# Weights in DRAM by tap column: long writes and short reads in a convolution with involution

## The chip, the cores and the metric

The kernel runs on one core of a Trainium2 chip. The metric is the device time of one execution in microseconds, lower being better. The number to be predicted is the median over runs of the changed kernel.

## The reference

The input x has 32 images of 256 channels and 32 x 32 pixels. Two layers follow each other, each added to its own input:

```python
# layer 0: 3x3 convolution over group-normalised x, quantised to 10 mantissa bits
x = x + conv3x3(quantise(gn(x)), quantise(w0)) + bias
# layer 1: involution, 7x7, 16 groups of 16 channels
xn = gn(x)
y = relu(bn(w1 @ xn))             # 64 channels
w = w2 @ y + b2                   # per pixel: 16 groups x 49 taps
x = x + sum over k of w[g, k] * patch(xn)[g, c, k]
```

The second layer has different weights at every pixel, made from that pixel itself. `gn` has 32 groups of 8 channels.

## The kernel before

An image passes through five stages.

1. `front` normalises it, runs the 3x3 convolution in float16 on TensorE (L320, 18 matmuls for each half of the pixels and of the channels), adds bias and input on VectorE, normalises again into `xn` (L269), multiplies by w1 into PSUM (`py`, L368), and ScalarE turns that into `y_sb` (L375), which holds one image in one of two buffers. Then it transposes `xn` pixel by channel (L383) into `pixels`.
2. `weights` multiplies y by w2 for four rows of pixels at a time (L398). VectorE adds b2 and writes the result into the ring `w_sb` (L416). There, a partition is a pixel's column (and a pair of tap columns), and the free dimension runs over image rows, groups and tap rows.
3. `scatter` writes the weights from `w_sb` to the DRAM buffer `wd`, one DMA for each of the seven tap columns and each block of eight rows (L465, on SyncE's queue). `wd` is laid out by row and pixel: a pixel's weights for all seven tap columns lie together, so a DMA writes runs of WB = 160 floats, 640 bytes.
4. `load_bands` reads `wd` back into one of three `band` buffers, so that the partition is now a pixel (eight rows by 16 columns). It takes 16 DMAs for each block of eight rows, one for each of 16 columns (L478); each reads runs of a whole pixel, WPIX = 1124 floats, 4496 bytes, for two sides of the image. One in eight goes to SyncE's queue, the others to GpSimd's (POOL in the profile).
5. `sums` multiplies `pixels` by `band` (L503). The result in `acc` is what each pixel gives to the 7x7 window around it, and `add_windows` adds it to x on VectorE (L519). `store` writes the finished half image (L524).

Sizes: K = 4 blocks of eight rows per image, SIDES = 2, JC = 16 columns to a side. WINC = 22 columns of weights stand in a band for 16 pixels, WINI = 19 of them inside the image.

The order is written out by hand. A loop runs over steps; an image has 16, two for each of its M = 8 pieces, and every stage is called at its distance from the sums. `front` is a generator that goes on by one `yield` per step, and it starts 56 steps ahead. `weights` comes 18 steps ahead, `scatter` 17, `load_bands` 9 steps. Engines take their instructions in that order, each its own. The DMAs of a queue use eight semaphores in turn, so that a DMA waits for the one eight before it on its queue to land.

Of the kernel before, what the change touches and what calls it, by code (L numbers as in the profile page):

```python
# [9 lines left out]
F32 = mybir.dt.float32  # L10
AF = mybir.ActivationFunctionType
ALU = mybir.AluOpType

P = 128
B, C, H, W = 32, 256, 32, 32
N = H * W
# [3 lines left out]
K0, PAD0 = 3, 1  # L20
K1, PAD1 = 7, 3
TAPS = K1 * K1
CR = 64
G = 16
# [12 lines left out]
XR = 4  # L37
RG = 2
KP = P // RG
TR = RG * XR  # L40
SIDES = 2
JC = W // SIDES
K = H // TR
M = K * SIDES
WIN = XR + K1 - 1
WINC = JC + K1 - 1
WINI = JC + PAD1

WB = G * WIN
WPIX = K1 * WB + XR
SW = K1 * G
S = H + 2 * PAD1
T = 4
TW = P // T
PAIR = 3 * GC
PAIRS = G // 2
ROW = S * WPIX  # L60
WR = 4
NBAND = 3
SHARE = 8
NPIX = 6
# [7 lines left out]
def tile_quant_conv_then_involution(  # L72
# [16 lines left out]
    nc = tc.nc  # L89
    PSUM = bass.MemoryType.PSUM  # L90

    const = ctx.enter_context(tc.tile_pool(name="const", bufs=1))
# [3 lines left out]
    dram = ctx.enter_context(tc.tile_pool(name="dram", bufs=1, space=bass.MemoryType.DRAM))  # L96
# [37 lines left out]
    for t in sum(sum(sums_sb, []), []):  # L134
        nc.gpsimd.memset(t, 0.0)

    y_sb = [const.tile([P, N // 2], F32, name=f"y_{i}") for i in range(2)]
    bands = [const.tile([P, SIDES, WINC * WB + XR], F32, name=f"band_{i}") for i in range(NBAND)]
    for t in bands[CH:]:
        nc.gpsimd.memset(t, 0.0)  # L140
    pixels = [const.tile([P, 2, PAIRS, PAIR], F32, name=f"pixels_{i}") for i in range(NPIX)]
# [3 lines left out]

    w_sb = const.tile([P, 2, RING, G, WIN], F32, name="w_sb")
    nc.vector.memset(w_sb, 0.0)  # L147
    wd = dram.tile([H, S, WPIX], F32, name="wd")
    acc = [ps_acc.tile([P, RG, NT], F32, name=f"acc_{d}") for d in range(SIDES)]

    wq = const.tile([P, CH, K0 * K0, C], F16, name="wq")
    for kh in range(CH):
        wf = bands[kh].rearrange("p d n -> p (d n)")[:, : K0 * K0 * C].rearrange("p (k c) -> p k c", c=C)
        nc.sync.dma_start(wf, w0[kh * P : (kh + 1) * P])
        nc.vector.tensor_scalar(wq[:, kh], wf, F16_MAX, -F16_MAX, ALU.min, ALU.max)
        nc.gpsimd.memset(bands[kh], 0.0)
# [20 lines left out]
    bn_scale = const.tile([P, 1], F32, name="bn_scale")  # L177
    nc.vector.tensor_mul(bn_scale, bn[:, 0:1], bn_r)
    bn_shift = const.tile([P, 1], F32, name="bn_shift")
# [1 line left out]
    nc.vector.tensor_sub(bn_shift, bn[:, 1:2], bn_shift)  # L181


    for col, cols, at, n in (
        (0, S, K1 * WB, XR),
        (PAD1, PAD1, 0, PAD1 * WB),
        (W, PAD1, (K1 - PAD1) * WB, PAD1 * WB),
    ):
        to = bass.AP(
            tensor=wd.tensor,  # L190
            offset=wd.offset + col * WPIX + at,
            ap=[[ROW, H], [WPIX, cols], [1, n]],
        )
        nc.sync.dma_start(to, bands[NBAND - 1][:H, 0, :n].unsqueeze(1).to_broadcast([H, cols, n]))

    class GroupNorm:

# [77 lines left out]
    def front(b):  # L275
# [4 lines left out]
        def stages(n):  # L280
            for _ in range(n):
                yield

        gn = GroupNorm(b, 0)
# [18 lines left out]
        gn = GroupNorm(b, 1)  # L303
        gn.begin(N // NT)
        units = [(nt, mh) for nt in range(N // NT) for mh in range(CH)]
        for s in range(4 * len(units) + 2):
            u, i = divmod(s, 4)
            if u < len(units):
# [3 lines left out]
                for n in range(sum(CONV[:i]), sum(CONV[: i + 1])):  # L312


                    k = n if n < K0 * K0 else CH * K0 * K0 - 1 - n
                    kh, k = n // (K0 * K0), (k + K0 * K0 // 2) % (K0 * K0)
                    di, dj = k // K0 - PAD0, k % K0 - PAD0
                    r0, r1 = max(nt * RT, -di), min((nt + 1) * RT, H - di)
# [9 lines left out]
            u, i = divmod(s - 3, 4)  # L328
            if 0 <= u < len(units) and i < 3:
                nt, mh = units[u]  # L330
                cols = slice(nt * NT, (nt + 1) * NT)
# [22 lines left out]
        for h in range(CH):  # L354
            yield
            to = xn[:, h].rearrange("p (k d r j) -> p d k r j", d=SIDES, r=TR, j=JC)
            at = xt[:, h].rearrange("p (k r d j) -> p d k r j", d=SIDES, r=TR, j=JC)
            gn.apply(h, [(to[:, d], at[:, d]) for d in range(SIDES)])
        yield from stages(2)

        py = ps_m.tile([P, NT], F32, tag="m", name="py")
        for r0 in range(0, H, WR):
            cols = slice(r0 // 2 * W, (r0 + WR) // 2 * W)
            for kh in range(CH):
                px = xn[:, kh].rearrange("p (k d r j) -> p k r d j", d=SIDES, r=TR, j=JC)[:, r0 // TR]
                for i in range(2):
                    r = r0 % TR + 2 * i
# [4 lines left out]
                        start=kh == 0,  # L372
                        stop=kh == CH - 1,
                    )
        nc.scalar.activation(y_sb[b % 2], py, AF.Relu, bias=bn_shift, scale=bn_scale)  # L375
        yield from stages(5)

        for m in range(0, M, 2):
            yield
# [6 lines left out]
            to = pixels[(b * M + m) // 2 % NPIX].rearrange("p i a (v c) -> p (i a) v c", c=GC)  # L386
# [3 lines left out]
    def weights(b, r0):  # L390

        pws = [ps_w.tile([P, 2, 2, SW], F32, tag=f"pw{i}", name=f"pw{i}") for i in range(2)]
        for r in range(2):
            for t in range(T):
                for i in range(2):
                    half = slice(i * CR, (i + 1) * CR)
                    dj = slice(2 * t, min(2 * t + 2, K1))
                    nc.tensor.matmul(  # L398
                        pws[i][t * TW : (t + 1) * TW, r, : dj.stop - dj.start],
                        y_sb[b % 2][half, (r0 // 2 + r) * W : (r0 // 2 + r + 1) * W],  # L400
                        w2_sb[half, dj],
                        start=True,
                        stop=True,
                    )
        for i in range(2):
            for e in range(2):
                p = P if e == 0 else (K1 // 2) * TW
                for r, rows, d0, d1, at in ring_pieces(b, r0 + 2 * i):

                    to = w_sb[:p, e]  # L410
                    to = bass.AP(
                        tensor=to.tensor,
                        offset=to.offset + at * WB + K1 - 1 - d0,
                        ap=[to.ap[0], [WB, rows], [WB - 1, d1 - d0], [WIN, G]],
                    )
                    nc.vector.tensor_tensor(  # L416
                        to,
                        pws[i][:p, r : r + rows, e, d0 * G : d1 * G].rearrange("p r (d g) -> p r d g", g=G),
                        b2_sb[:p, e, d0 * G : d1 * G]
                        .unsqueeze(1)  # L420
                        .to_broadcast([p, rows, (d1 - d0) * G])
                        .rearrange("p r (d g) -> p r d g", g=G),
                        ALU.add,
                    )
# [29 lines left out]
    def scatter(b, k):  # L454

        at = (b * H + k * TR) % RING
        for dj in range(K1):
            t, e = divmod(dj, 2)
            to = bass.AP(
                tensor=wd.tensor,  # L460
                offset=wd.offset + k * TR * ROW + dj * WPIX + (K1 - 1 - dj) * WB,
                ap=[[WPIX, TW], [ROW, TR], [1, WB]],
            )
            rows = w_sb[t * TW : (t + 1) * TW, e, at : at + TR]
            nc.sync.dma_start(to, rows.rearrange("p s g r -> p s (g r)"))  # L465

    def load_bands(b, k):

        band = bands[(b * K + k) % NBAND]
        for i in range(JC):  # L470
            j = i // 2 + i % 2 * JC // 2
            src = bass.AP(
                tensor=wd.tensor,
                offset=wd.offset + k * TR * ROW + (j + PAD1) * WPIX,
                ap=[[ROW - 1, TR], [JC * WPIX, SIDES], [1, WPIX]],
            )
            queue = nc.sync if i % SHARE == SHARE - 1 else nc.gpsimd
            queue.dma_start(band[j::JC, :, j * WB : j * WB + WPIX], src)  # L478

    def windows(b, m):  # L480

# [7 lines left out]
    def sums(b, m):  # L489

        k, d = divmod(m, SIDES)
        j0 = 0 if d else PAD1
        band = bands[(b * K + k) % NBAND][:, d]
        px = pixels[(b * K + k) % NPIX][:, d]
        for h in range(CH):
            for v in range(2):
                for g, at, top, f, l in windows(b, m):
                    p = slice(g * KP, (g + 1) * KP)
                    of = band[p, g * XR + j0 * WB : g * XR + (j0 + WINI) * WB]
                    of = of.rearrange("p (j g r) -> p j g r", g=G, r=WIN)  # L500
                    for t in range(T):
                        a = h * T + t
                        nc.tensor.matmul(  # L503
                            at[t * TW : (t + 1) * TW, h, :, f - top : l - top],
                            px[p, a, v * GC : v * GC + TW],
                            of[:, :, 2 * a + v, f - top : l - top],
                            start=(h, v) == (0, 0),
                            stop=(h, v) == (CH - 1, 1),
                        )
# [25 lines left out]
    with tc.manual_schedule():  # L535
        fronts = {}
        for n in range(FRONT, B * per + 2):
            b, i = due(n, FRONT)
# [10 lines left out]
            b, i = due(n, 0)  # L549
            if b is not None and i % 2 == 0:  # L550
                sums(b, i // 2)
            b, i = due(n, 1)
# [6 lines left out]
            b, i = due(n, 2)  # L559
            if b is not None and i == 2 * (M - 1 - SIDES):  # L560
                store(b, 0)
            b, i = due(n, -LEAD)
# [3 lines left out]
            b, i = due(n, -LEAD + 1)  # L566
# [4 lines left out]
            b, i = due(n, LOAD)  # L571
# [3 lines left out]
            b, i = due(n, 3 - 4 * NBAND)  # L575
# [39 lines left out]
```

## Time and profile before

| | |
|---|---|
| median of 3 runs | 1402.68 us (1398.28 to 1410.33) |
| profiled execution | 1416.45 us |
| its span | 1414.7 us |
| granted TensorE clock, mean | 0.978 |
| TensorE busy | 1265.2 us (89%) |
| VectorE busy | 933.0 us (66%) |
| ScalarE busy | 729.8 us (52%) |
| GpSimd (POOL) busy | 1003.5 us (71%) |
| moved by DMA | 369.33 MB in 366232 packets |

In the profile PE is TensorE, PEld its loading of weights, DVE VectorE, ACT ScalarE, POOL GpSimd, SP SyncE. L478 is line 478 of the kernel. A q behind an engine means its queue, which waits and issues. In the table of DMA queues, q1 is what SyncE issues (scatters, an eighth of the band loads, loads and stores of x), and q0 is what GpSimd issues (the other band loads). Each line gives packets, megabytes, and the time that the packets took as a share of the time of all 16 DMA engines. A wait is given as who waited for whom, with the total in microseconds, the number of times and the longest.

### The profile page before, as it was taken

How to read it: one execution, taken by the hardware profiler on the slowest of the kernel's cores; microseconds unless marked ns; L12 is line 12 of the kernel's file. 1: busy time of each engine (PE TensorE's matmuls, PEld its weight loads, DVE VectorE, ACT ScalarE, POOL GpSimd, SP SyncE). 2: the span in 40 equal slices, each digit the busy share in tenths (PEclk: the TensorE clock that was granted, in tenths of full speed). 3: DMA queues.
4: the chain of work that ended last, by engine and by line, in shares of the span. 5: the costliest groups of instructions: out<-in, count | busy, mean ns of one | idle time of the engine just before them, and what ended most of it. 6: DMA issues, size and time to landing. Idle time of an engine off the chain costs nothing.

```text
span 1414.7 us, 70076 instructions
## 1 busy us (share of the span) xinstructions
PE 1265.2 (89%) x29440; PEld 802.2 (57%) x29440; DVE 933.0 (66%) x3180; ACT 729.8 (52%) x1699; POOL 1003.5 (71%) x1817
## 2 busy tenths in 40 slices
PE   4899899999999899989999999999999999999665
PEld 1456565566565566655566556565566556655543
DVE  4567667767677677766767667767667676766642
ACT  5775555455555445555545555554556454553300
POOL 7067767686776777767777777677776767777774
PEclk9999999999999999999999999999999999999976
DMA  6099899999999999999999999999999999999995
GB/s 212 6 228 283 251 277 276 281 262 285 277 273 264 287 268 269 294 260 270 289 267 287 268 277 253 273 280 273 274 289 271 268 279 282 278 270 262 258 258 165
DMA packets 366232, 369.33 MB, mean 261 GB/s; under 512 B 78624, under 2 KB 308192, under 8 KB 365664
## 3 DMA queue, kind: packets, MB, share of 16 engines
q1 hardware_dynamic: 279904, 235.72, 57.2%
q0 software_dynamic: 86016, 129.14, 34.5%
q8 instruction: 234, 3.83, 1.2%
q14 instruction: 78, 0.64, 0.1%
HBM read 183.81 MB, written 180.74 MB: 258 GB/s over the span
## 4 chain that ended last, share of the span: by engine, by line
PE 47%; DMA 31%; issue 7%; POOL 5%; DVE 4%; ACT 3%; SPq 2%; POOLq 0%; DVEq 0%; ACTq 0%
DMA band<-wd 24%; PE pc L320 19%; PE acc L503 15%; PE pw L398 9%; DMA wd<-w_sb 7%; POOL band L478 5%; PE py L368 3%; DVE w_sb L416 2%; PE pt L383 2%; SPq L465 2%; ACT junk L210 1%; DVE x L519 0%; DVE w_sb L147 0%; ACT xn L269 0%; DVE q L334 0%
## 5 line engine op out<-in xcount | busy, mean ns | idle before, releaser
L478 POOL DMA_DIRECT2D band<-wd x1792 | 978.0, 548 | 397.8 <-DMA band<-wd 249.0
L416 DVE TENSOR_TENSOR w_sb<-pw,b_sb 128x16 f32<-128x16 f32 (+9 forms) x1920 | 454.0, 350 | 386.9 <-PE pw L398 363.2
L320 PE MATMUL pc<-xq,wq 128*128 128x496 f16 (+3 forms) x2304 | 536.5, 379 | 31.3 <-ACT xq L269 21.4
L503 PE MATMUL acc<-band,pixels 64*32 64x190 f32 (+1 forms) x16384 | 420.5, 323 | 78.9 <-DMA band<-wd 39.6
L503 PEld LDWEIGHTS acc<-band,pixels 64*32 64x32 f32 x16384 | 298.3, 108 | 171.1 <-issue 101.5
L320 PEld LDWEIGHTS <-wq 128*128 128x128 f16 x2304 | 206.4, 98 | 328.9 <-issue 114.6
L398 PE MATMUL pw<-w_sb,y 64*32 64x224 f32 (+1 forms) x8192 | 296.6, 333 | 31.1 <-issue 29.4
L519 DVE TENSOR_TENSOR x<-acc,x 128x380 f32<-128x380 f32 (+1 forms) x512 | 261.7, 511 | 35.7 <-PE acc L503 26.8
L398 PEld LDWEIGHTS pw<-w_sb,y 64*32 64x32 f32 x8192 | 182.8, 107 | 63.0 <-issue 43.9
L387 ACT COPY pixels<-pt 128x512 f32<-128x512 f32 x128 | 73.6, 575 | 238.2 <-PE pt L383 238.2
L210 ACT ACTIVATE junk<-x 128x512 f16<-128x512 f32 (+1 forms) x192 | 146.5, 763 | 20.7 <-DVE x L336 15.2
L210 ACT ACTIVATE junk<-x,mean 128x1024 f16<-128x1024 f32 x128 | 147.1, 1149 | 4.3
L241 ACT ACTIVATE s<-back,eps 128x2 f32<-128x2 f32 x64 | 18.9, 296 | 193.7 <-DVE back L226 193.6
L334 DVE TENSOR_SCALAR q<-pc 128x512 f16<-128x512 f32 x128 | 87.2, 682 | 16.5 <-PE pc L320 16.3
L269 ACT ACTIVATE xn<-x,off,rstd 128x512 f32<-128x512 f32 x128 | 96.1, 799 | 0.0
L336 DVE SCALAR_TENSOR_TENSOR x<-q,bias_sb,x 128x512 f32<-128x512 f16 x128 | 92.1, 719 | 0.2
L383 PEld LDWEIGHTS pt<-ident,xn 128*128 128x128 f32 x512 | 64.0, 142 | 27.4 <-issue 3.2
L383 PE MATMUL pt<-ident,xn 128*128 128x128 f32 x512 | 78.1, 275 | 0.9 <-ACT pixels L387 0.9
L231 ACT ACTIVATE mean<-back 128x2 f32<-128x2 f32 x64 | 12.7, 199 | 127.6 <-DVE back L226 127.6
L269 ACT ACTIVATE xq<-x,off,rstd 128x1024 f16<-128x1024 f32 x64 | 75.8, 1227 | 0.1
L368 PEld LDWEIGHTS py<-xn,w_sb 128*64 128x64 f32 x2048 | 63.0, 139 | 16.5 <-issue 8.1
L368 PE MATMUL py<-xn,w_sb 128*64 128x64 f32 x2048 | 67.8, 224 | 2.3 <-ACT xn L269 1.8
(40 smaller groups left out, 370.7 us busy)
## 6 DMA issues: line engine op xcount, KB each, us to landing
wd<-w_sb SPq DMA_DIRECT2D x896, 160.0 KB
band<-wd POOLq DMA_DIRECT2D x1792, 70.2 KB
x<-in_x SPq DMA_DIRECT2D x64, 512.0 KB
out<-x SPq DMA_DIRECT2D x64, 512.0 KB
band<-wd SPq DMA_DIRECT2D x256, 70.2 KB
band<-in_w SPq DMA_DIRECT2D x2, 1152.0 KB
w_sb<-in_w SPq DMA_DIRECT2D x2, 196.0 KB
wd<-band SPq DMA_DIRECT2D x2, 180.0 KB
```

The costliest lines, as they stand in the source:

```text
L210: nc.scalar.activation(junk[:, n0:n1], src[:, h, n0:n1], func, bias=bias, accum_out=self.sums[:, i : i + 1])
L269: nc.scalar.activation(dst, src, AF.Identity, bias=self.off[:, one], scale=self.rstd[:, one])
L320: nc.tensor.matmul(pc.rearrange("p (r c) -> p r c", c=W)[:, r0 - nt * RT : r1 - nt * RT, c0:c1], wq[:, kh, k, mh * P : (mh + 1) * P], xq[: ...
L334: nc.vector.tensor_scalar(q, pc, F16_MAX, -F16_MAX, ALU.min, ALU.max)
L336: nc.vector.scalar_tensor_tensor(xt[:, mh, cols], q, bias_sb[:, mh : mh + 1], xt[:, mh, cols], ALU.add, ALU.add)
L368: nc.tensor.matmul(py[i * CR : (i + 1) * CR, cols], w1_sb[:, kh, :], px[:, r : r + 2], start=kh == 0, stop=kh == CH - 1,)
L383: nc.tensor.transpose(pt[:, i, h * P : (h + 1) * P], xn[:, h, (m + i) * P : (m + i + 1) * P], ident)
L398: nc.tensor.matmul(pws[i][t * TW : (t + 1) * TW, r, : dj.stop - dj.start], y_sb[b % 2][half, (r0 // 2 + r) * W : (r0 // 2 + r + 1) * W], w ...
L416: nc.vector.tensor_tensor(to, pws[i][:p, r : r + rows, e, d0 * G : d1 * G].rearrange("p r (d g) -> p r d g", g=G), b2_sb[:p, e, d0 * G : d ...
L478: queue.dma_start(band[j::JC, :, j * WB : j * WB + WPIX], src)
L503: nc.tensor.matmul(at[t * TW : (t + 1) * TW, h, :, f - top : l - top], px[p, a, v * GC : v * GC + TW], of[:, :, 2 * a + v, f - top : l - top],
L519: nc.vector.tensor_tensor(x_at, of, x_at, ALU.add)
```

## The change

The DRAM buffer `wd` is laid out the other way round: by block of eight rows, then tap column, then pixel column, and only then by the eight rows. What one partition of `w_sb` holds of a tap column for eight rows now lies together in DRAM, RUN = 1280 floats, 5120 bytes, and a scatter writes 32 such runs where it wrote 256 of 640 bytes. A band load, which wants one row's weights from all seven tap columns, now finds these in seven places for each side. It reads 7 x 2 runs per row of WBP = 164 floats, 656 bytes, 112 in all where there were 16 of 4496 bytes. The number of DMAs is the same, and so is the share of the queues.

The other edits follow from it. A tap column gets 33 slots, of which the last holds zeros (one DMA at the start in place of three). The layout needs the pixel columns in reverse, so `xn` is written with columns and sides reversed. The band buffers are ordered by column, then side, and grow from 7048 to 7216 floats per partition. In exchange `y_sb` has one buffer instead of two, and the step that fills it comes one step later (`stages(3)` and `stages(4)` for `stages(2)` and `stages(5)`). `sums` reads the band with another stride; its matmuls keep their shapes.

```diff
-WPIX = K1 * WB + XR
+WBP = WB + XR
+RUN = TR * WB
+SLOT = W + 1
...
-    y_sb = [const.tile([P, N // 2], F32, name=f"y_{i}") for i in range(2)]
-    bands = [const.tile([P, SIDES, WINC * WB + XR], F32, name=f"band_{i}") for i in range(NBAND)]
+    y_sb = const.tile([P, N // 2], F32, name="y")
+    bands = [const.tile([P, WINC, SIDES, WBP], F32, name=f"band_{i}") for i in range(NBAND)]
...
-    wd = dram.tile([H, S, WPIX], F32, name="wd")
+    wd = dram.tile([K, K1, SLOT, RUN], F32, name="wd")
...
-            gn.apply(h, [(to[:, d], at[:, d]) for d in range(SIDES)])
-        yield from stages(2)
+            gn.apply(h, [(to[:, SIDES - 1 - d], at[:, d, :, :, ::-1]) for d in range(SIDES)])
+
+        yield from stages(3)
...
-        nc.scalar.activation(y_sb[b % 2], py, AF.Relu, bias=bn_shift, scale=bn_scale)
-        yield from stages(5)
+        nc.scalar.activation(y_sb, py, AF.Relu, bias=bn_shift, scale=bn_scale)
+        yield from stages(4)
...
-                offset=wd.offset + k * TR * ROW + dj * WPIX + (K1 - 1 - dj) * WB,
-                ap=[[WPIX, TW], [ROW, TR], [1, WB]],
+                offset=wd.offset + (k * K1 + K1 - 1 - dj) * SLOT * RUN,
+                ap=[[RUN, TW], [1, RUN]],
...
-                offset=wd.offset + k * TR * ROW + (j + PAD1) * WPIX,
-                ap=[[ROW - 1, TR], [JC * WPIX, SIDES], [1, WPIX]],
+                offset=wd.offset + (k * K1 * SLOT + j + PAD1) * RUN,
+                ap=[[WB - 1, TR], [JC * RUN, K1 * SIDES], [1, WBP]],
             )
+            c = JC - 1 - j
             queue = nc.sync if i % SHARE == SHARE - 1 else nc.gpsimd
-            queue.dma_start(band[j::JC, :, j * WB : j * WB + WPIX], src)
+            queue.dma_start(band[j::JC, c : c + K1].rearrange("p c d n -> p (c d) n"), src)
...
-        band = bands[(b * K + k) % NBAND][:, d]
-        px = pixels[(b * K + k) % NPIX][:, d]
+        band = bands[(b * K + k) % NBAND][:, j0 : j0 + WINI, SIDES - 1 - d]
+        px = pixels[(b * K + k) % NPIX][:, SIDES - 1 - d]
...
-                    of = band[p, g * XR + j0 * WB : g * XR + (j0 + WINI) * WB]
-                    of = of.rearrange("p (j g r) -> p j g r", g=G, r=WIN)
+                    of = band[p, :, g * XR : g * XR + WB].rearrange("p j (g r) -> p j g r", r=WIN)
```

More of the change, by code (lines that the diff above doesn't have):

```diff
@@ L52 @@
 WB = G * WIN
-WPIX = K1 * WB + XR
+WBP = WB + XR
+RUN = TR * WB
+SLOT = W + 1
 SW = K1 * G
-S = H + 2 * PAD1
 T = 4
@@ L59 @@
 PAIRS = G // 2
-ROW = S * WPIX
 WR = 4
@@ L152, in tile_quant_conv_then_involution @@
     for kh in range(CH):
-        wf = bands[kh].rearrange("p d n -> p (d n)")[:, : K0 * K0 * C].rearrange("p (k c) -> p k c", c=C)
+        wf = bands[kh].rearrange("p c d n -> p (c d n)")[:, : K0 * K0 * C].rearrange("p (k c) -> p k c", c=C)
         nc.sync.dma_start(wf, w0[kh * P : (kh + 1) * P])
@@ L181, in tile_quant_conv_then_involution @@
     nc.vector.tensor_sub(bn_shift, bn[:, 1:2], bn_shift)
[L184 to L194, printed above, removed]
+    to = bass.AP(
+        tensor=wd.tensor, offset=wd.offset + W * RUN, ap=[[SLOT * RUN, K * K1], [RUN // TR, TR], [1, WB]]
+    )
+    nc.sync.dma_start(to, bands[NBAND - 1][: K * K1, 0].rearrange("p d n -> p (d n)")[:, :WB].unsqueeze(1).to_broadcast([K * K1, TR, WB]))
     class GroupNorm:
@@ L399, in weights @@
                         pws[i][t * TW : (t + 1) * TW, r, : dj.stop - dj.start],
-                        y_sb[b % 2][half, (r0 // 2 + r) * W : (r0 // 2 + r + 1) * W],
+                        y_sb[half, (r0 // 2 + r) * W : (r0 // 2 + r + 1) * W],
                         w2_sb[half, dj],
@@ L460, in scatter @@
                 tensor=wd.tensor,
-                offset=wd.offset + k * TR * ROW + dj * WPIX + (K1 - 1 - dj) * WB,
-                ap=[[WPIX, TW], [ROW, TR], [1, WB]],
+                offset=wd.offset + (k * K1 + K1 - 1 - dj) * SLOT * RUN,
+                ap=[[RUN, TW], [1, RUN]],
             )
             rows = w_sb[t * TW : (t + 1) * TW, e, at : at + TR]
-            nc.sync.dma_start(to, rows.rearrange("p s g r -> p s (g r)"))
+            nc.sync.dma_start(to, rows.rearrange("p s g r -> p (s g r)"))
     def load_bands(b, k):
```

## The prediction

> **What bounds the kernel now.** I read the page's table of engines first, then its queues, then the steady stretch from 100 to 1300 us by engine, then the waits there, and last the short stretches in which one kind of transfer runs alone. The profiled execution took 1416.45 us, of which the span is 1414.7. The median of the runs shown is 1402.68, so I work in the profiled execution and multiply by 0.990 at the end.
>
> The queues on the page (packets, MB, share of the 16 DMA engines' time):
>
> ```profile
> DMA packets 366232, 369.33 MB, mean 261 GB/s; under 512 B 78624, under 2 KB 308192, under 8 KB 365664
> q1 hardware_dynamic: 279904, 235.72, 57.2%
> q0 software_dynamic: 86016, 129.14, 34.5%
> ```
>
> With the instruction queues (1.3%) the DMA engines are taken for 93.0% of the span, 1316 us. The stretches show how that divides (PE, PEld, DVE, ACT, POOL busy, clock, DMA share, GB/s):
>
> ```profile
> 400.00:600.00 200.00, 188.29 (x4486) 120.39 (x4485) 137.29 (x462) 110.21 (x259) 146.65 (x270) 0.99 0.97 275
> 1340.00:1380.00 40.00, 27.16 (x762) 19.36 (x756) 20.21 (x69) 2.34 (x4) 32.41 (x61) 0.78 0.94 258
> ```
>
> Two things are nearly full at once: the DMA engines at 97 to 98% and TensorE at 94%. In the tail TensorE falls off and the DMA engines do not, so there the transfers alone set the pace. Summed over 100 to 1300 us, TensorE is busy 1120 of 1200 us. Freeing the DMA engines can thus win at most the 80 idle us there and a little of the tail; loading them further costs time almost one for one.
>
> POOL is the third. Its waits between 100 and 1300 us (us in total, times, longest):
>
> ```profile
> POOL band L478 <- DMA band<-wd: 226.8, 293, 2.9
> POOL band L478 <- DMA wd<-w_sb: 21.5, 33, 2.7
> ```
>
> and its load in the view of line 478 (shortest, median and longest in ns):
>
> ```profile
> L478 POOL DMA_DIRECT2D band<-wd x1792: 547/547/683, 77.3 to 1401.3; - x200
> ```
>
> POOL mostly waits for earlier band loads to land (each load waits for the one eight before it). Its own work is a constant 547 ns per load, 882 us or 73% of the steady stretch; minimum and median agree, so these are not stalls.
>
> **What a packet costs.** Three stretches hold one kind alone: x loads of 4096 bytes, output stores of 2048, and at the end band loads with no scatter left to issue.
>
> ```profile
> q1 hardware_dynamic: 355, 1.28, 104.2%
> q1 hardware_dynamic: 272, 0.52, 34.7%
> q0 software_dynamic: 960, 1.44, 47.9%
> ```
>
> The first (28.5 to 31.5 us): 312 data packets in 1.042 x 3 x 16 = 50.0 engine-us, about 159 ns each. The second (1411 to 1415 us): 256 packets in 22.2 engine-us, 86 ns. The line through both is 13 ns + 0.0356 ns per byte: 36 ns for 640 or 656 bytes, 173 for 4496, 195 for 5120. Bands cost more than this line. On the whole page q0's 488 us x 16 / 28672 is 272 ns per 4496 bytes with its two 4-byte packets; without those (13 each by the line) 246, a factor of 1.42. In the third stretch (1392 to 1404 us) it is 287, less 26: 261, a factor of 1.51, with the scatters over. So the excess is not the scatters' doing; it belongs to reading bands into few partitions at a time. Small reads show it too: between 12 and 14 us 187 or so packets of 448 bytes take some 40 ns where the line says 29, a factor of 1.38.
>
> Scatters do not show it: q1's 809 us, less 70 for SyncE's eighth of the bands, 81 to 120 for x (I take 100), 89 for the output and some 20 of set-up, leave 530 us, 37 ns per packet of 640 bytes.
>
> **What the Trainium skill says.** "DMA: Bandwidth & Descriptors", section "Why small descriptors are slow (HBM only)": each packet carries a fixed overhead beside its bytes. The trace agrees; here it is about 13 ns, a third of a 656-byte packet. The same page, "Anatomy of one DMA": generating descriptors is small, and many can be emitted before the extra cost shows. No view here tests that, since all of POOL's loads have 16 data packets. "Perfetto Trace Analysis", section "DMA Instruction — SWDGE (GPSIMD)": the recorded end of a GpSimd DMA is when the last core has written its descriptors. That makes the 547 ns a price of generation and not of moving data, as its constancy beside landings of 3 to 7 us supports. "SBUF — State Buffer", section "A bandwidth-pool intuition that's wrong (but worth ruling out)", gives a GpSimd DMA about 620 ns alone, without its shape.
>
> **The change, part by part.**
>
> *Scatters.* Still 896 DMAs and the same 146.8 MB, but 28672 packets of 5120 bytes for 229376 of 640. At 195 ns and the scatters' own small excess (37/36): 200 ns x 28672 / 16 = 358 us for 530. Minus 172 us of DMA engine time.
>
> *Band loads.* Still 2048 DMAs. Each had 8 rows x 2 sides = 16 runs of 4496 bytes and has 8 x 14 = 112 of 656: 229376 packets for 32768, 150.5 MB for 147.3. Before: 246 ns x 32768 / 16 = 504 us. After, bounded from both sides: at the bare line 36 ns, 516 us (plus 12); with the third stretch's 1.51, 54 ns, 774 us (plus 270). I take the lowest factor seen on a read, 1.38[...]: 50 ns, 717 us, plus 213. The 4-byte packets stay.
>
> *Sum for the DMA engines:* -172 + 213 = +41 us, between -160 and +98. At 98% occupancy, 41/0.98 = +42 us of span.
>
> *POOL.* 1792 loads, each now with 96 more data packets to generate. Lower bound: nothing more, 547 ns. Upper bound: a tiny memset on POOL takes 93 ns, so at most 454 ns go to the 48 packets recorded per load, 9.5 each: 547 + 96 x 9.5 = 1459 ns. POOL hides the load as long as it stays below 1200 us / 1616 loads = 743 ns. I take 620 to 700 ns from the skill's two statements, 1110 to 1250 us in all, hidden beside the transfers; cost zero. The cover is thin: at 800 ns POOL sets the pace.
>
> *SyncE.* Its 896 scatters take 302 to 2448 ns to issue, median 620, while x loads of 128 packets take 423. With 32 long packets the scatters should need no more than that; SyncE's 256 band loads (766 ns) get dearer with 112 packets. SyncE is in order, so the x loads, stores and next scatters stand behind both; the saving of some 0.2 us x 896 covers 0.7 us x 256. Zero.
>
> *y in one buffer, a stage later.* The 64 matmuls into py and the activation move one step, behind the last weight matmuls that read the old y. Before the first weight matmuls of the new image there still stand 9 matmuls of the 3x3 convolution (2.0 us) and the acc matmuls (1.45 us); the activation takes 0.78 and follows at once in the trace. Zero; if ScalarE's queue were late, at most about 1 us x 32.
>
> *Reversed columns, acc's new stride, two set-up DMAs fewer.* Matmul, activation and add counts and shapes are the same. A negative step on ScalarE's read and a longer step on TensorE's are not seen in this trace; I take zero, bounds -5 to +20 us. The set-up DMAs lie beside the first image's work.
>
> Forecast: 1416.45 + 42 = 1458, times 0.990 is 1444 us.
>
> **Rivals.**
>
> *Faster: the small reads escape the excess.* If a run of 656 bytes moves at 36 to 40 ns, bands take 516 to 574 us, and the DMA engines lose 102 to 160 us, 8 to 12%. They then cease to bind; TensorE does. Of its 80 idle us two thirds might go, with some 6 in the tail: 1416 - 59 = 1357, times 0.990 = 1344 us. For it: the reads' excess came with long packets[...]. Against it: the 448-byte reads had the excess too. It decides below 47 ns per packet, where -172 is just balanced.
>
> *Slower by far: POOL becomes the bound.* Halfway between its bounds a load costs 1.0 us: 77 + 1792 x 1.0 + 14 = 1883, times 0.990 = 1865 us. For it: POOL is already at 73% and seven times the runs must be written by software. Against it: the skill's 620 ns. It decides from 743 ns.
>
> *Nothing to measure.* At 46 to 48 ns the two changes cancel: 1403 us.
>
> **How the numbers follow.** DMA engines loaded further: 0.40, its own range 1417 to 1510 us (48 to 54 ns, plus the unseen strides). Faster: 0.30. POOL the bound: 0.18. Cancelled: 0.12. A measurement of this kernel can tell about 1% from no change, so: faster 0.30, same 0.12, slower 0.58. The range runs from 1335, just under the faster case, to 1700, where POOL's load would cost 907 ns; beyond it I leave about half of the POOL case and a small part of the faster one.
>
> **What would show it.** The queues should show q1 with some 104000 packets and q0 with about 258000; q0's share should grow from 34.5% to about 46%, q1's fall from 57.2% to about 46%. The POOL row should read 620 to 700 ns and leave idle time before it. TensorE's waits for band loads should grow. If q0's data packets are at 40 ns or less and TensorE rises above 95%, the forecast is wrong toward faster; if POOL's mean is over 743 ns with no idle time left, it is wrong toward much slower.

## The result and the profile after

The changed kernel took 1453.2 us at the median (1450.18 to 1458.22, 4 runs), the kernel before 1404.34 us. The ratio is 1.035, 95% interval 1.030 to 1.041: slower, as forecast, and within 1% of the 1444 us forecast. The parts of the sum behind it came out otherwise, and the experiments were about that. (The kernel before has one more run here than in the table above.) The profiled execution took 1450.18 us, its span 1448.4.

The queues on the page of the changed kernel (packets, MB, share of the 16 DMA engines' time):

```profile
DMA packets 188886, 372.92 MB, mean 257 GB/s; under 512 B 77374, under 2 KB 106270, under 8 KB 188318
q1 hardware_dynamic: 102558, 235.87, 52.6%
q0 software_dynamic: 86016, 132.58, 36.1%
```

With the instruction queues (1.2%) that is 89.9% of 1448.4 us, 1302 us of engine time, where the kernel before had 1316. Engine time is here the time that all packets took, divided by 16. The transfers did not get heavier in sum; they got 14 us lighter. GpSimd's queue still has 86016 packets. 132.58 MB over its 28672 long packets is 4624 bytes, that is seven runs of 656 (4592) and a small remainder: seven runs of a GpSimd load are recorded as one packet. On SyncE's queue each run stays a packet of its own, and q1's 102558 are near the 104000 that were forecast.

The steady stretch by engine (PE, PEld, DVE, ACT, POOL busy, clock, DMA share, GB/s), then GpSimd's load in the view of its line (shortest, median, longest in ns):

```profile
400.00:600.00 200.00, 179.74 (x4251) 115.55 (x4238) 134.35 (x449) 107.29 (x251) 151.58 (x262) 0.99 0.95 272
1380.00:1420.00 40.00, 24.88 (x680) 17.87 (x680) 16.85 (x60) 1.17 (x2) 32.21 (x56) 0.71 0.92 262
```

```profile
L475 POOL DMA_DIRECT2D band<-wd x1792: 584/584/733, 75.4 to 1434.5; - x200
```

TensorE fell from 94% to 90% busy here, and the DMA engines fell too, from 97% to 95%. GpSimd writes a load's descriptors in 584 ns where it took 547: seven times the runs cost it 37 ns. Its waits from 100 to 1300 us, beside those of the kernel before (us in total, times, longest):

```profile
POOL band L475 <- DMA band<-wd: 201.9, 245, 4.2
POOL band L475 <- DMA wd<-w_sb: 21.0, 35, 2.5
```

GpSimd waits some ten times as long for its own earlier loads as for the scatters, in both kernels. Between 100 and 1300 us it was busy for 907 us and waited 202 for loads of its own, 1109 of 1200, as before (882 + 227). In that time it issued 1569 loads where it had issued 1616: 765 ns for each instead of 743. The semaphore records of the traces also tell how long a load takes from its issue to its landing: 5.11 us on average before and 5.36 now.

### The profile page after: what moved, and what is told of

The parts are those of the page before. It is cut to its first block, busy times and chain, and to the rows that moved or that the text cites. A ratio compares the mean times of both kernels' runs of the same rounds, so it can differ in the third digit from the quotient of the medians.

```text
span 1448.4 us, 70074 instructions
## 1 busy us (share of the span) xinstructions
PE 1266.6 (87%) x29440; PEld 807.3 (56%) x29440; DVE 933.6 (64%) x3180; ACT 730.2 (50%) x1699; POOL 1062.9 (73%) x1817
## 3 DMA queue, kind: packets, MB, share of 16 engines
q1 hardware_dynamic: 102558, 235.87, 52.6%
q0 software_dynamic: 86016, 132.58, 36.1%
## 4 chain that ended last, share of the span: by engine, by line
PE 50%; DMA 26%; issue 6%; POOL 6%; DVE 6%; SPq 4%; ACT 2%; POOLq 0%; DVEq 0%; ACTq 0%
PE pc L315 19%; DMA band<-wd 16%; PE acc L499 16%; PE pw L394 10%; DMA wd<-w_sb 8%; POOL band L475 6%; SPq L461 4%; PE py L364 4%; DVE w_sb L412 3%; PE pt L379 2%; ACT junk L205 1%; DMA out<-x 1%; DVE x L515 1%; DMA x<-in_x 0%; DVE w_sb L149 0%
## 5 line engine op out<-in xcount | busy, mean ns | idle before, releaser
L475 POOL DMA_DIRECT2D band<-wd x1792 | 1037.0, 585 | 371.6 <-DMA band<-wd 217.5
L499 PE MATMUL acc<-band,pixels 64*32 64x190 f32 (+1 forms) x16384 | 421.3, 324 | 95.8 <-DMA band<-wd 55.8
L394 PE MATMUL pw<-w_sb,y 64*32 64x224 f32 (+1 forms) x8192 | 291.7, 332 | 24.5 <-issue 21.6
L371 ACT ACTIVATE y<-py,bn_shift,bn_scale 128x512 f32<-128x512 f32 x32 | 24.8, 776 | 151.2 <-PE py L364 151.2
L364 PE MATMUL py<-xn,w_sb 128*64 128x64 f32 x2048 | 72.7, 227 | 21.2 <-issue 20.6
L364 PEld LDWEIGHTS py<-xn,w_sb 128*64 128x64 f32 x2048 | 66.2, 141 | 35.1 <-issue 33.4
```

Of the source, the lines that this page charges most:

```text
L364: nc.tensor.matmul(py[i * CR : (i + 1) * CR, cols], w1_sb[:, kh, :], px[:, r : r + 2], start=kh == 0, stop=kh == CH - 1,)
L394: nc.tensor.matmul(pws[i][t * TW : (t + 1) * TW, r, : dj.stop - dj.start], y_sb[half, (r0 // 2 + r) * W : (r0 // 2 + r + 1) * W], w2_sb[ha ...
L475: queue.dma_start(band[j::JC, c : c + K1].rearrange("p c d n -> p (c d) n"), src)
L499: nc.tensor.matmul(at[t * TW : (t + 1) * TW, h, :, f - top : l - top], px[p, a, v * GC : v * GC + TW], of[:, :, 2 * a + v, f - top : l - top],
```

## The experiments

Times are ratios to the kernel before, measured beside it on the same chip, with 95% intervals. A line of dots in a diff stands for lines left out.

**y alone.** `y_sb` is one buffer and is filled one step later; nothing else.

```diff
-        yield from stages(2)
+        yield from stages(3)
...
-        nc.scalar.activation(y_sb[b % 2], py, AF.Relu, bias=bn_shift, scale=bn_scale)
-        yield from stages(5)
+        nc.scalar.activation(y_sb, py, AF.Relu, bias=bn_shift, scale=bn_scale)
+        yield from stages(4)
```

> The kernel before with only the edit to y: one buffer for y, filled one step later; reads and writes of the weights as before. Theory 'short reads cost DMA time' (the prediction's): y is free, so ratio to before 1.00, within 0.5%. Rival 'the later py': ScalarE's waits for py were 127 us in the steady stretch of the changed kernel and 29 us in all before; if that delay reaches TensorE, this kernel alone is 2 to 3.5% slower.

Measured: 1.002 (0.999 to 1.005). ScalarE's wait for py from 100 to 1300 us is nearly as long here as in the changed kernel (127.2 us; 22.0 us before), so that wait costs nothing that can be told from noise. This kernel's line among the waits:

```profile
ACT y L375 <- PE py L368: 114.5, 29, 7.3
```

**Long writes alone.**

```diff
-                offset=wd.offset + k * TR * ROW + dj * WPIX + (K1 - 1 - dj) * WB,
-                ap=[[WPIX, TW], [ROW, TR], [1, WB]],
+                offset=wd.offset + k * TR * ROW + (K1 - 1 - dj) * W * RUN,
+                ap=[[RUN, TW], [1, RUN]],
...
-                ap=[[ROW - 1, TR], [JC * WPIX, SIDES], [1, WPIX]],
+                ap=[[K1 * W * RUN // TR - 40, TR], [JC * WPIX, SIDES], [1, WPIX]],
```

> The kernel before with only the scatters changed: runs of 5120 bytes into a block of eight rows; band loads still read 16 runs of 4496 bytes of the same block, in places that no longer belong to their pixels (the output is not the reference's). Theory 'short reads cost DMA time': the scatters save DMA time and nothing is added, so 2 to 4% faster than before. Rival 'long writes cost': a packet of 5120 bytes took 249 ns on average in the changed kernel and not 200, and holds up what stands behind it; then equal to before or slower by 1 to 3%.

Measured: 0.987 (0.983 to 0.991), a gain between the ranges of the two theories. The queues on its page, span 1386.0 us, and its steady stretch:

```profile
q1 hardware_dynamic: 79200, 235.72, 52.0%
q0 software_dynamic: 86016, 129.14, 33.8%
100.00:1300.00 1200.00, 1131.87 (x26990) 723.03 (x26989) 840.09 (x2891) 655.67 (x1538) 901.24 (x1646) 0.99 0.91 278
```

With 1.4% for instructions the engines have 1209 us, 107 less than before, and the time falls by 18. The packet records of the trace give the 5120-byte packets 436 us, 243 ns each on average and not 200; the 640-byte packets before had 519. So 83 us of the 107 are the scatters' own, and 18 are the band loads', whose unchanged packets of 4496 bytes fell from 253 to 243 ns.

The excess over the prediction's line (195 ns) is not peculiar to these 32 partitions or to the bands. Half of the 5120-byte packets took 196 ns or less, the line's price; the others pull the average up. The x loads show the same: alone, in the stretch through which the line was drawn, their 4096-byte packets take 159 ns each, and from 100 to 1300 us of the kernel before they take 223 on average and 166 at the median. Stores of 2048 bytes hardly differ (86 and 89 ns). Other traffic is not the whole of it: in the prediction's third stretch, with the scatters over, the bands' packets of 4496 bytes still average 269 ns (median 187). What makes some long packets slow, no run isolates.

**Short reads alone.**

```diff
-                ap=[[ROW - 1, TR], [JC * WPIX, SIDES], [1, WPIX]],
+                ap=[[ROW + 137, TR], [WPIX, K1 * SIDES], [1, WBP]],
...
```

> The kernel before with only the band loads changed: 112 runs of 656 bytes where there were 16 of 4496, from places of the same block that do not all belong to their pixels (the output is not the reference's); scatters still write 640 bytes. Theory 'short reads cost DMA time': plus 213 us of DMA engine time by the prediction's sum, that is over 10% slower. Read by the changed kernel's profile, in which the bands took only about 50 us of engine time more: 3 to 5% slower. Rival 'the later py' or 'long writes cost': equal to before within 1%.

Measured: 1.062 (1.055 to 1.069). Its queues, span 1501.9 us, and its steady stretch:

```profile
q1 hardware_dynamic: 304480, 236.11, 57.7%
q0 software_dynamic: 86016, 132.58, 36.7%
100.00:1300.00 1200.00, 1069.13 (x24840) 676.19 (x24838) 774.69 (x2673) 613.33 (x1431) 877.37 (x1511) 0.98 1.00 260
```

95.6% with the instructions: 1436 us of engine time, 120 more than before. By the packet records 79 us of this are the bands' own, and 29 the scatters', whose unchanged packets of 640 bytes went from 36 to 38 ns. Here the DMA engines are the bound, with 100% of the steady stretch.

**Both, with two buffers for y.** The writes of the second kernel and reads as in the changed one:

```diff
...
+                ap=[[WB - 1, TR], [JC * RUN, K1 * SIDES], [1, WBP]],
...
```

> Long writes and short reads together, with two buffers for y and py where it was, columns not reversed (the runs read do not belong to their pixels; the output is not the reference's). If the transfers explain the change, this is 3 to 4% slower than before, as the changed kernel is (1.035). If the later py explains it, equal to before within 1%.

Measured: 1.031 (1.027 to 1.035). The transfers explain the change: what they leave to y, the reversed columns and the strides, 0.4%, lies within the intervals. But they do it with no more engine time than before. The queues, and the steady stretch:

```profile
q1 hardware_dynamic: 103776, 236.11, 53.2%
q0 software_dynamic: 86016, 132.58, 35.6%
100.00:1300.00 1200.00, 1100.23 (x25800) 696.20 (x25785) 806.49 (x2801) 634.45 (x1484) 911.38 (x1570) 0.99 0.94 270
```

90.0% of 1448.1 us is 1303, as against 1316. What did grow is the time from issue to landing of a GpSimd load: 5.38 us on average, where it was 5.11 before, 4.95 with long writes alone and 5.62 with short reads alone. Of the two edits, 107 us of engine time taken from the scatters are worth 18 us of time, and 120 us added to the band loads cost 89. On the other base, too: from short reads alone to both, the scatters give back 133 us of engine time for 46 of time, and from long writes alone to both the loads add 94 for 62. Part of the first pair was to be expected: with TensorE 93% busy before, freed engine time can win little, while added engine time has no such limit.

**Where the loads are issued.** Two theories for what engine time leaves open: SyncE's loads, of eight rows each, crowd eight of the engines; or GpSimd's queue, with eight loads on the way, sets the pace. The first rests on the Trainium skill ("DMA: Bandwidth & Descriptors", section "Why a DMA increments its semaphore by 16 and not by 1"): a DMA runs on the largest number of engines up to 16 that divides the outermost sizes of its two sides, so 8 for eight rows and 16 for sixteen, and from SyncE on the lowest-numbered ones. No view here shows which engine a packet took. First no loads on SyncE, then a quarter (`SHARE = 17`, `SHARE = 4`), on the changed kernel.

> The changed kernel with all 16 band loads of a block on GpSimd's queue, none on SyncE's. Theory 'eight full engines': a SyncE band load has 8 rows and so, by the skill, runs on the lowest 8 of the 16 DMA engines; those 8 carry all of SyncE's 87 us (mean over 16), that is 174 each, and set the time. Without them every engine has about 1290 us: 2 to 4% faster than the changed kernel (1.00 to 1.015 of before). Rival 'eight loads in flight': GpSimd may have 8 loads on the way and a landing takes 5.4 us, so 56 loads an image are at least 38 us and 64 are 43: 3 to 8% slower than the changed kernel (1.07 to 1.12).

Measured: 1.129 (1.124 to 1.135), 9% slower than the changed kernel. TensorE then waits for band loads, 125 us from 100 to 1300 us where the changed kernel had 25:

```profile
PE acc L499 <- DMA band<-wd: 125.2, 64, 5.9
POOL band L475 <- DMA band<-wd: 185.0, 207, 3.3
100.00:1300.00 1200.00, 1019.89 (x23467) 658.43 (x23457) 736.70 (x2541) 583.04 (x1359) 943.88 (x1634) 0.96 0.87 246
```

Here neither the DMA engines (87%) nor TensorE (85%) are full, and GpSimd issues loads or waits for its own loads to land for 944 + 185 = 1129 of 1200 us. In this kernel its queue sets the pace, although a load lands sooner than in the changed kernel (4.88 us on average, not 5.36).

> The changed kernel with a quarter of the band loads on SyncE's queue instead of an eighth. Theory 'eight full engines': these loads put 87 us more (mean) on DMA engines that are already full, so 4 to 8% slower than the changed kernel (1.08 to 1.12 of before). Rival 'eight loads in flight': GpSimd has 48 loads an image instead of 56, so 2 to 4% faster than the changed kernel (1.00 to 1.015).

Measured: 1.096 (1.090 to 1.103), slower as well. So each theory was about right for one of these two kernels. Next, SyncE's loads as 16 rows of half as many runs, first at an eighth, in the changed kernel and in the one before:

```diff
...
+                    ap=[[74, 2 * TR], [JC * RUN, K1], [1, WBP]],
...
+                to = band[j % 8 :: 8].rearrange("p c d n -> p (c d) n")[:, :K1]
+                nc.sync.dma_start(to, src)
...
```

> The changed kernel with SyncE's band loads in another shape: 16 partitions of 7 runs of 656 bytes in place of 8 partitions of 14 runs, as many bytes and packets, in places that don't belong to their pixels (the output is not the reference's). Such a load can use all 16 DMA engines. Theory 'eight full engines': 3 to 5% faster than the changed kernel (0.985 to 1.01 of before). Rival 'eight loads in flight' and the prediction's 'mean engine time': equal to the changed kernel within 1% (1.025 to 1.045).

Measured: 1.029 (1.024 to 1.034).

> The kernel before with SyncE's band loads as 16 partitions of one run of 4496 bytes in place of 8 partitions of two, as many bytes and packets, in places that don't belong to their pixels (the output is not the reference's). Theory 'eight full engines': the lowest eight lose 65 us, and the kernel before is 1 to 3% faster (0.97 to 0.99), then bound by TensorE. Rivals: equal to before within 1%.

Measured: 0.997 (0.994 to 0.999). At an eighth, the shape of SyncE's loads is worth 0.3 to 0.6%, in both kernels: eight full engines are not what the change costs. The same shape with a quarter on SyncE:

> The changed kernel with a quarter of the band loads on SyncE's queue, these in the shape of 16 partitions of 7 runs, which can use all 16 DMA engines (runs that do not belong to their pixels; the output is not the reference's). Theory 'GpSimd's queue of loads is the pace' (14 loads of a block take it 10.3 of the 10.7 us from block to block): with 12 loads it needs about 9 us, so faster than the changed kernel by 3 to 6%, down to what TensorE allows (0.98 to 1.00 of before). The slowness of a quarter in the real shape (1.096) is then the lower eight DMA engines'. Rival 'SyncE's queue': a quarter is slow because SyncE issues short runs slowly; then about as slow again (1.07 to 1.10).

Measured: 1.038 (1.033 to 1.042). Neither range held. Against 1.096 in the real shape, the shape was most of the harm of a quarter, as eight crowded engines would have it. But GpSimd, with two loads a block fewer, gives nothing back. The short runs on SyncE travel singly, and the DMA engines are now full:

```profile
100.00:1300.00 1200.00, 1101.41 (x25488) 688.64 (x25479) 796.96 (x2754) 632.98 (x1472) 767.03 (x1325) 0.99 0.99 266
```

> The kernel before with a quarter of the band loads on SyncE's queue, in the shape of 16 partitions of one run of 4496 bytes (runs that do not belong to their pixels; the output is not the reference's). Theory 'GpSimd's queue of loads is the pace': the kernel before is paced by it too (10.1 of 10.4 us), so 1 to 3% faster than before, then bound by TensorE or by DMA engine time. Rival 'mean DMA engine time': the same bytes on the same engines, equal to before within 1%.

Measured: 1.055 (1.048 to 1.061), against both theories. The waits suggest that more loads in SyncE's order delay the scatters behind them: before it writes `w_sb`, VectorE waits 180 us for transfers from 100 to 1300 us, where it waited 15 before. TensorE then waits for VectorE, its longest wait, which in the kernel before was 1.0 us in all:

```profile
PE pw L398 <- DVE w_sb L416: 65.3, 46, 4.9
```

**GpSimd's own work.** The kernel before, with idle work in its queue:

```diff
             queue.dma_start(band[j::JC, :, j * WB : j * WB + WPIX], src)
+            if i in (0, 2, 5, 8, 10, 13):
+                nc.gpsimd.memset(idle, 0.0)
```

> The kernel before with six memsets of one element per partition on GpSimd between the 14 band loads of a block, about 0.56 us a block, nearly what the change adds to writing the descriptors (14 x 37 ns = 0.52 us); the transfers are those of before. Theory 'GpSimd's queue is the pace, through the time of its own work': 3 to 5% slower than before. Rival 'GpSimd's queue is the pace, through the landings': the memsets fall into its waits for landings (1.8 us a block), so 0 to 1.5% slower. If GpSimd is not the pace: equal within 0.5%.

Measured: 1.003 (1.001 to 1.005). In GpSimd's groups from 100 to 1300 us, 82 us of memsets have come in, and the waits for loads fell from 227 to 204:

```profile
L479 POOL DMA_DIRECT2D band<-wd x1618 | 884.5, 548 | 278.6 <-DMA band<-wd 203.5 <-issue 38.5 <-DMA wd<-w_sb 16.6
L481 POOL MEMSET idle<- 128x1 f32 x693 | 81.7, 118 | 0.0
```

At 118 ns six of them are 0.7 us a block, more than the 14 x 37 = 0.5 us of the change. The first theory's 3 to 5% did not come: on the kernel before, as much work as the change adds to writing descriptors costs 0.3%. The other two theories both allow this, so the run does not tell them apart; nor does it test a kernel with long writes, whose DMA engines leave GpSimd more room.

**The number of runs.** The fourth kernel with 56 runs of 1312 bytes a load:

```diff
-                ap=[[WB - 1, TR], [JC * RUN, K1 * SIDES], [1, WBP]],
+                ap=[[WB - 1, TR], [SIDES * JC * RUN, K1], [1, SIDES * WBP]],
...
```

> As the kernel with long writes and short reads and two buffers for y (1.031 of before), but each band load reads 56 runs of 1312 bytes instead of 112 of 656, as many bytes (runs that do not belong to their pixels; the output is not the reference's). Long writes with 16 runs of 4496 bytes gave 0.987. Theory 'a price for every run read': the cost follows the number of runs, 0.987 + 0.044 x 40/96 = 1.005 of before, and a load lands between the two. Rival 'not the number of runs but reading seven tap columns at once, or the longer band layout': about 1.03 as with 112 runs.

Measured: 1.010 (1.005 to 1.014), the middle between 16 runs (0.987) and 112 (1.031). Its queues, span 1427.1 us, and its load on GpSimd:

```profile
q1 hardware_dynamic: 89440, 236.11, 51.3%
q0 software_dynamic: 86016, 132.18, 34.1%
L481 POOL DMA_DIRECT2D band<-wd x1792: 582/582/715, 81.4 to 1413.4; - x200
```

With the writes held and the bytes nearly so, the time rises with the number of runs. The engine time does so less evenly: 1209, 1236 and 1303 us. A load's landing lengthens mostly in the second step (4.95, 5.03 and 5.38 us on average), GpSimd's own time for it mostly in the first (550, 582 and 587 ns). So writing descriptors is not what costs the 2% from 56 to 112 runs; for the step from 16 to 56 no run excludes it.

## Why the prediction was right or wrong

*What bounds the kernel.* The DMA engines and TensorE were named as both nearly full, and that held: with long writes alone the engines' share falls to 91% and TensorE, 94% busy, is the fuller of the two; with short reads alone the engines are the bound. The prediction also said that freed engine time could win little and added engine time would cost nearly all of itself. What it had not seen is the third limit. It weighed GpSimd's own work against 743 ns a load and took the waits for landings as room; with no loads on SyncE, GpSimd's queue is the bound without any more work in a load. And it added scatters and bands into one sum and turned that into time one for one. The runs say 0.17 to 0.34 us of time per us of engine time for scatters, and 0.66 to 0.74 for band loads. The waits of the kernel before already hinted at it: GpSimd waited 227 us for its own loads and 22 for scatters. A load's landing lets the next load go and lets TensorE begin; the scatters have mostly landed by the time GpSimd gets to them. How much of the difference is this, and how much TensorE's limit, the runs do not separate.

*Scatters, minus 172 us.* Measured alone: minus 107, of which 83 are theirs. The term that failed is the price of the long packet: 243 ns, and 249 in the changed kernel, not 200. The prediction took it from stretches in which one kind of transfer runs alone and gave it the small excess of the 640-byte packets. In the steady stretch long packets of every kind cost more than that on average, x loads too, so the excess did not belong to "reading bands into few partitions at a time" alone.

*Band loads, plus 213 us.* Measured alone: plus 120, of which 79 are their long packets'; in the changed kernel these add 50. SyncE's single packets of 656 bytes took 48 ns on average, so the price of 50 was right for them, though it was reached from 448-byte packets read as 40 ns, which the packet records put at 36. But seven of eight loads have no such packets: q0's 523 us over 28672 groups of seven runs are 292 ns, 42 a run with the small packets inside, and 38 without them. The rival's 36 to 40 ns was close for these, and in sum the engines did get lighter, by 14 us. Yet neither its 102 to 160 us of saving nor its time, 1344 us, came.

So both terms were too large by 65 and 93 us, and their errors nearly cancelled. Measured alone they sum to +13 us and measured together to -14, against the +41 predicted. That the time came within 1% all the same is luck: 41 us of engine time at one for one stood in for a loss that came with no more engine time at all.

*POOL.* Taken at 620 to 700 ns, measured 584; the upper bound of 1459 was far off, and the rival in which GpSimd's own work becomes the bound is excluded. The idle time before it stayed. The Trainium skill ("DMA: Bandwidth & Descriptors", section "Anatomy of one DMA") says that many descriptors can be emitted before it shows, and the trace agrees: 37 ns for 96 runs more, 0.4 ns for each. That they cost nothing is shown for the kernel before (0.3% by the memsets) and not for the changed one.

*y.* Zero, shown alone (1.002). *SyncE.* The issue of scatters went from 620 to 512 ns at the median, that of its band loads from 766 to 778. These medians fit the zero; no run isolates this term.

*What the profile should have shown.* q0's share grew to 36.1%, not 46%, with 86016 packets, not 258000. q1's fell to 52.6%, not 46%. TensorE's waits for band loads grew (39.6 to 55.8 us on the page), and POOL kept idle time. The direction was right; the packet counts would have told that the sum was not.

*What stays open.* Why a load of many runs costs time beyond its packets. Its packets as recorded explain part: with 56 runs the engines have 80 us less than in the kernel before, and it is still 1% slower. The set of engines is excluded at an eighth. Descriptors written by GpSimd are excluded for the step from 56 to 112 runs, and as the whole cost on the kernel before. What is left is inside the DMA engines between packets, and the time at which loads land, which did lengthen (5.11 to 5.36 us). How many loads may be on the way, eight, was not varied, so that GpSimd's window sets the price in the changed kernel is argued from its waits and not shown.

## What to carry to other kernels

Do not add all transfers into one sum of DMA engine time: long writes and short reads together left the sum as it was and cost 3%. Ask of each kind who waits for it. In this kernel a us of engine time taken from transfers that land early was worth a third or less, with TensorE nearly full too, and one added to those that release the next issue about two thirds to three quarters. When a layout trades the run length of writes against that of reads, look first at giving the long runs to the side that somebody waits for; here these were the reads, and the kernel before had them so. And price a packet in the steady stretch, not where its kind runs alone.

## What the runs showed of the hardware

GpSimd's loads of 14 short runs per row were recorded as packets of seven runs (4592 bytes) on its queue, 268 ns on average, while SyncE's stayed single at 656 bytes and 48 ns. A load of seven times the runs took GpSimd 584 ns to issue instead of 547. The same packet of 4096 bytes took 159 ns while x loads ran alone and 223 on average in the steady stretch of the kernel before; a write packet of 5120 bytes took 243 to 249 ns on average, although the line through 2048 and 4096 bytes says 195. And of the three shares of the loads on SyncE that were tried in the changed kernel, an eighth was the best: none gave 1.129, a quarter 1.096, an eighth 1.035.
